# Head, last items and end of a 32-item attention and graph-convolution kernel: values, x loads, a scaling and additions rearranged

## The chip, the cores and the metric

The kernel runs on one core of a Trainium2 chip. A core has five engines that run their own instruction queues beside each other: TensorE (PE, with weight loads shown apart as PEld), VectorE (DVE), ScalarE (ACT), GpSimd (POOL) and SyncE (SP), which here only issues DMAs. The metric is the device time of one execution in microseconds, the median of several. Times of instructions come from one profiled execution.

## The reference

For 32 items x of 512 nodes by 512 features, and one 512x512 adjacency, two layers, each with a residual and a layer normalisation:

```python
q, k, v = x @ Wq + bq, x @ Wk + bk, x @ Wv + bv          # 8 heads of 64
scores  = einsum('bihd,bjhd->bhij', q, k) / 8 + mask     # -1e9 where adj == 0
out     = einsum('bhij,bjhd->bihd', softmax(scores), v)
x       = layernorm(x + out)
...
norm_adj = adj * deg_inv_sqrt[:, None] * deg_inv_sqrt[None, :]
x       = layernorm(x + norm_adj @ (x @ weight) + bias)
```

All is float32.

## The kernel before

**Products.** The three 512x512 products of an item with weights (values; keys and queries; the convolution) are made with seven half-size products instead of eight, from sums of blocks. A table such as `CHAIN` (L322) lists the seven: the bank of PSUM to multiply into, the two blocks, and what to do then: `put` a bank to its place (ACT copies) or `add` it there (DVE). `seven` (L357) turns a table into seven steps. Where it is done at two levels (`quarters_of`, L407), seven products of quarter blocks (matmuls with 128 columns) take the place of one of the seven, and three further ones (`OUTER`) have 256 columns. The quarter sums of x lie in the tail of the buffer `XT` (`xT` in the profile), made by POOL; those of the weights are in `wv_quarters` and `w1_quarters`, made by `weigh_quarter` (L255), whose fourth operation overwrites a quarter of the weights themselves.

**An item.** For item b of the loop at L898: `stretch` (L526) makes scores and numerators of one half of the heads (32 matmuls `sc`; DVE masks and clips, ACT exponentiates, POOL sums them into `acc`), then their values (`av`, 32 matmuls). DVE transposes each `av` into the single buffer `yb` (L514), and SP stores it in four DMAs to `yT` (L521). Then come the keys and queries of item b+1, the load of the value weights into `wqv` (`swap(1)`, L264; the same buffer holds the query weights and the value weights in turn), a second `stretch`, the loads of x of item b+2 (`load_x`, L123), and a stage of values of item b+1 (`values_of`, L379) together with the convolution of item b-1 (`convolve`, L706); at its end `swap(0)` loads the query weights. In the first turn there is no convolution yet, so the stage of values of item 1 stands alone. `finish` (L586) holds layer 0's end: `inverse` (1/sum), `scale` (DVE, one row block of 512 at a time) or `scale_head` (ACT, one head at a time), `add` of the residual, `measure` (statistics), `root`, `norm`, `low`, `lift`, `grow`. `fold` (L540) turns the sums `acc` on DVE. `turn` (L131) transposes x into `XT` on DVE; `combine` makes its block differences on POOL.

**Order.** DVE, ACT, POOL and PE run in the order of the program: `InOrder` (L35) pins it, and so the profile names L45 for all of them. The program writes that order by hand with `play` (L106): a list of main steps, and a dictionary of what is to be issued after which step. SP's DMAs aren't pinned: the framework places them among the others, and SP then runs its queue strictly in that order. Tiles have a fixed number of buffers in pools; a new tile waits until the old one's readers are done.

**The ends.** Item 1's weights at the start are in `wv` (part of the numerators' buffer) and are stored once to DRAM (`stored[1]`, `wv_parts` in the profile), from where `swap(1)` loads them. For the last items the schedule differs: the stage of item 30 (`b == LAST - 1`) makes the convolution of item 29 with one level (`second`), its statistics and `low` of item 30 already in that stage. After the loop follow the convolutions of items 30 and 31. In the one of item 30 the seven products are copied aside, and POOL adds them to their places later (`move`, L800; the list `extend`).

Lines the change touches: L255 to L261 `weigh_quarter`, L401 in `values_of`, L883 to L891 before the loop, L905 the first `stretch`, L926 and L937 what is beside keys and queries, L961 to L998 the stage of values, L1016 to L1019 the end.

Of the kernel before, what the change touches and what calls it, by code (L numbers as in the profile page):

```python
# [10 lines left out]
F32 = mybir.dt.float32  # L11
# [7 lines left out]
P = 128  # L19
# [31 lines left out]
def unshifted(  # L51
# [54 lines left out]
    def play(main, beside=None):  # L106
        for n, f in enumerate(main):
            f()
            run((beside or {}).get(n, ()))
# [21 lines left out]
    def turn(b, j):  # L131
        vector.transpose(
            XT[:, 2 * j : 2 * j + 2].rearrange("p i u (k s) -> p (i u) k s", s=32),
            X.pop((b, j)).rearrange("p k t r -> p t k r"),
        )
# [116 lines left out]
    w1_quarters = consts.tile([P, 3, 4, P], F32, name="w1_quarters")  # L252
    stored = [drams.tile([P, 7, 2, HALF], F32, name=f"{name}_parts") for name in ("wq", "wv", "w1")]

    def weigh_quarter(w, new, at, engine):  # L255
        old = w[:, 1:5].rearrange("p k u (r o) -> p k u r o", r=2)
        to, a, c, op = (
            (new[:, 0], old[:, :, 0, 1], old[:, :, 1, 1], ALU.add), (new[:, 1], new[:, 0], old[:, :, 0, 0], ALU.subtract),
            (new[:, 2], old[:, :, 0, 0], old[:, :, 0, 1], ALU.subtract), (old[:, :, 0, 1], old[:, :, 1, 0], new[:, 1], ALU.subtract),
        )[at]  # L260
        engine.tensor_tensor(to, a, c, op)  # L261

# [116 lines left out]
    def values_of(b):  # L379
        w = wqv if b else wv  # L380

        def multiply(p, i, j, fresh):
            for r in range(2):
                for u in range(2):
                    tensor.matmul(
                        p[:, r, :], XT[:, j, u, ts(r, P)], w[:, i, u, :],
                        start=fresh and r == 0 and u == 0, stop=u == 1, skip_group_check=True,
                    )

        def out(i, j):  # L390
            if b not in V:
                V[b] = acts.tile([P, NT, D], F32, name="v", bufs=1)
            return V[b][:, 2 * j : 2 * j + 2, ts(i, HALF)]

        def put(q, p):
            scalar.copy(out(*q), p)

        def add(q, p):
            vector.tensor_add(out(*q), out(*q), p)

        if b == 0:  # L401
            return seven(PLAIN_FIRST, multiply, put, add)
        left = lambda k, s: XT[:, s, k % 2, ts(k // 2, P)] if k in (0, 1, 3) else QUARTERS[:, max(k - 3, 0), s - 1]
        leaf, _ = quarters_of(left, w, wv_quarters, lambda: V[b], lambda: out(0, 0))
        return leaf, lambda: gpsimd.tensor_add(out(0, 1), out(0, 1), out(1, 1)), seven(OUTER, multiply, put, add)
# [474 lines left out]
    wq_parts = each(lambda k: weigh_part(wqv, vector, k), *range(4))  # L880
    kq = keys_and_queries(0, 0)
    run(wq_parts[:2] + kq[:1] + wq_parts[2:3] + kq[1:2] + wq_parts[3:] + kq[2:])
    for k in range(4):  # L883
        weigh_quarter(wv, wv_quarters, k, gpsimd)
    gather(first_rows, rows(bv))
    nc.sync.dma_start(stored[1], NUM[:, :4].rearrange("p e k (u o) -> p (e k) u o", u=2)[:, :7])
    nc.sync.dma_start(stored[0], wqv)
    play(keys_and_queries(0, 1), {
        1: [lambda: adjacency(0)], 3: [lambda: turn(1, 0), lambda: adjacency(1)],
    })  # L890
    turn(1, 1)  # L891
    for k in range(4):
        combine(1, k)

# [3 lines left out]
    for b in range(B):  # L898
# [3 lines left out]
        if b == LAST - 1:  # L902
            nc.sync.dma_start(w1[:, 1:5, 0, P:], stored[2][:, 1:5, 0, P:])
        biased = []
        stretch(b, one, back["measure"][:3] if back else ())  # L905

        def folds(gs):
            return [[lambda g=g, b=b: fold(b, g)] for g in gs]
# [9 lines left out]
        if b < LAST:  # L918
            k0, k1 = keys_and_queries(b + 1, 0), keys_and_queries(b + 1, 1)
            main = [p for pair in zip(k0, k1) for p in pair]  # L920
            if b == 0:
                exact = each(compare, *range(NT))
                weights = each(lambda k: weigh_part(w1, gpsimd, k), *range(4))
                beside = {
                    1: fold0, 2: [degrees], 3: weights[:1], 4: fold1, 5: weights[1:2] + exact[:1], 6: exact[1:2],
                    7: weights[2:3], 8: exact[2:3], 9: weights[3:], 10: exact[3:], 11: [quarters],  # L926
                    12: each(lambda k: weigh_quarter(w1, w1_quarters, k, gpsimd), *range(3)),
                }
            else:
                measure, norm, low = ahead["measure"], ahead["norm"], ahead["low"]  # L930
                loads = [lambda b=b: biased.extend(load_residual(b))]
                scale = ahead["inverse"] + ahead["scale"] if b == 1 else []
                beside = {
                    0: rest + scale + ahead["add"], 1: store[:1] + fold0, 2: store[1:2], 3: store[2:3] + fold1,
                    4: store[3:] + measure[:2] + (loads if b == LAST - 1 else []), 5: measure[2:] + ahead["root"] + [quarters],
                    7: norm[:1] + ahead["judge"], 8: norm[1:2] + low[:1] + ([lambda: run(biased)] if b == LAST - 1 else []),
                    9: norm[2:3] + low[1:2] + (loads if b < LAST - 1 else []), 10: norm[3:] + low[2:3],  # L937
                    11: low[3:] + ahead["lift_all"],
                }
            play(main, beside)  # L940
            if b == 0:
                nc.sync.dma_start(stored[2], w1)
        else:
            e = f[b]
            conv = c[b - 1]
            play(conv["first"], {
                0: rest + store[:1] + conv["parts"][:0], 1: store[1:2] + ahead["judge"] + conv["parts"][:1],
                2: store[2:] + e["sums0"],
                3: conv["parts"][1:] + e["inverse0"] + ahead["grow"],
            })  # L950
# [9 lines left out]
            load_x(b + 2, 1)  # L960
        if b < LAST:  # L961
            end = f[b]
            leaf, spread_last, outer = values_of(b + 1)
            v = leaf[:6] + outer[:1] + leaf[6:] + [spread_last] + outer[1:]
            if b == 0:
                play(v, {
                    1: fold0, 4: fold1, 9: turn0 + [lambda: weigh_quarter(w1, w1_quarters, 3, gpsimd)],
                    10: turn1 + combined[:2], 11: combined[2:] + [lambda: swap(0)],
                })
            else:  # L970
                conv = c[b - 1]
                if b < LAST - 1:
                    leaf, outer = conv["leaf"], conv["outer"]
                    main = (
                        conv["first"] + v[:10] + leaf[:6] + outer[:1] + leaf[6:] + outer[1:2] + [conv["spread_last"]]
                        + v[10:11] + outer[2:3] + v[11:] + outer[3:]
                    )
                else:
                    second = conv["second"]
                    main = conv["first"] + v[:10] + second[:1] + v[10:11] + second[1:2] + v[11:] + second[2:]  # L980
                grow, parts, scale, heads = ahead["grow"], conv["parts"], end["scale"], end["scale_heads"]
                if b < LAST - 1:
                    beside = {
                        1: parts[:1] + fold0 + grow[:2], 2: grow[2:], 3: parts[1:] + conv["unjoin"] + conv["quarters"] + fold1,
                        5: end["inverse"], 7: heads[:14], 11: heads[14:23], 13: conv["open"], 16: turn0,
                        17: heads[23:], 19: conv["join"] + turn1, 20: combined[:1] + biased[:], 24: combined[1:2],
                        26: combined[2:] + [lambda: swap(0)],
                        27: [lambda: run(conv["extend"])],
                    }
                else:  # L990
                    measure, norm, low = end["measure"], end["norm"], end["low"]
                    biased = load_residual(LAST)
                    beside = {
                        1: parts[:1] + fold0, 3: parts[1:] + fold1, 5: end["inverse"], 6: grow[:1],
                        9: grow[1:2] + scale[3:], 11: grow[2:3] + scale[:1], 13: grow[3:] + scale[1:3] + end["add"],
                        16: measure[:2], 17: measure[2:3] + measure[3:] + end["root"],
                        18: norm[:1], 19: norm[1:2] + low[:1], 20: norm[2:3] + low[1:2] + biased,
                        21: norm[3:] + low[2:3], 22: low[3:] + end["lift"],  # L998
                    }
                play(main, beside)  # L1000

# [11 lines left out]
        0: end["sums1"] + end["turn_values"] + end["inverse1"], 1: whole[0], 2: whole[1] + halves[:1], 3: whole[2],  # L1013
        4: whole[3] + halves[1:] + norm[:1], 5: low[:1] + norm[1:2], 6: low[1:2] + norm[2:3],
    })
    run(block[:1] + norm[3:] + low[2:3] + block[1:2] + low[3:] + block[2:] + end["lift"] + held["extend"])  # L1016
    run(e["unload"] + e["parts"] + end["grow"])
    s, tail, halves = e["second"], held["measure"][2:] + held["root"] + held["store"], e["halves"]
    run(s[:2] + halves[0] + s[2:4] + held["measure"][:2] + end["judge"])  # L1019
    vector.tensor_reduce(count, FINE, AX.X, ALU.add)  # L1020
    run(s[4:5] + tail[:3] + s[5:6])

# [290 lines left out]
```

## Time and profile before

| | us |
|---|---|
| median of 3 runs | 2726.34 (2726.14 to 2730.94) |
| the profiled execution | 2729.19, of which its span 2727.4 |
| first `stretch` of item 0 begins | 49.44 |
| values of item 1 (28 matmuls of 128 columns, 12 of 256) | 103.24 to 123.64 |
| an item in the middle (from one second stretch to the next) | 83.45 |
| its keys and queries; its values and convolution | 24.37; 30.9 |
| stage of values with item 30 | 2602.93 to 2635.84 |
| from the last `av` matmuls' end to the end of the span | 2674.64 to 2727.4 |

The span begins at the first instruction and ends with the last. A row of a timeline is a start, a length, an engine, a line, an operation with its output and inputs, and how often it ran in a row; in brackets stands how long the engine was idle before and what it waited for. A PE row's length includes the modelled end of its last matmul, so that rows can overlap. A float32 matmul gives two records in the trace.

### The profile page before, as it was taken

The numbers are of one execution on the slowest core, as the hardware profiler recorded it, in microseconds if no ns is written. First come the engines' busy times: TensorE is split into PE (matmuls) and PEld (weight loads), VectorE is DVE, ScalarE is ACT, GpSimd is POOL, SyncE is SP. The second block draws the span as 40 slices with busy tenths as digits, with TensorE's granted clock in tenths as the row PEclk, the third lists the DMA queues.
The fourth block names the chain that finished last, engine by engine and source line by source line (L and its number), as shares of the span: only waits on it lengthen the run. The fifth ranks groups of instructions, "written<-read, shape, count | busy, mean of one in ns | idle before, by whom it ended". The sixth has DMA issues, their size and how long they took to land. (4 is left out here: it accounts for less than half of the span.)

```text
span 2727.4 us, 39255 instructions
## 1 busy us (share of the span) xinstructions
PE 2697.1 (99%) x13980; PEld 1914.4 (70%) x13980; DVE 1960.0 (72%) x2751; ACT 1515.8 (56%) x2793; POOL 2062.6 (76%) x1385
## 2 busy tenths in 40 slices
PE   9999999999999999999999999999999999999997
PEld 6676676766767767767667677677676676766765
DVE  4777767777777777767777777777767767777777
ACT  3355555565555655555655556555556555565554
POOL 5777787777787777877777877778777787777765
PEclk9999999999999999999999999999999999999999
DMA  6335444545345454444553454544545444445541
GB/s 185 109 92 145 121 108 114 119 128 128 104 114 139 105 141 117 106 124 112 137 126 103 116 138 106 134 117 101 132 111 140 122 106 113 122 125 128 127 90 44
DMA packets 421468, 323.79 MB, mean 119 GB/s; under 512 B 279825, under 2 KB 347921, under 8 KB 413073
## 3 DMA queue, kind: packets, MB, share of 16 engines
q1 hardware_dynamic: 387520, 254.88, 31.9%
q0 software_dynamic: 32736, 65.02, 14.9%
q8 instruction: 113, 1.85, 0.3%
q10 hardware_dynamic: 1008, 1.31, 0.2%
q14 instruction: 91, 0.74, 0.1%
HBM read 248.78 MB, written 39.06 MB: 106 GB/s over the span
## 5 line engine op out<-in xcount | busy, mean ns | idle before, releaser
L45 ACT ACTIVATE e<-e 128x1024 f32<-128x1024 f32 x512 | 541.0, 1057 | 128.4 <-DVE e L45 97.5
L45 POOL TENSOR_TENSOR acc<-acc,e 128x1024 f32<-128x1024 f32 x248 | 589.3, 2376 | 19.4
L45 DVE SCALAR_TENSOR_TENSOR e<-sc,maskT 128x1024 f32<-128x1024 f32 x512 | 584.9, 1214 | 19.7 <-PE sc L45 19.4
L45 PE MATMUL mm<-xT,wk 128*128 128x256 f32 x1792 | 464.5, 382 | 2.7 <-DVE kq L45 2.5
L45 PE MATMUL mm<-xT,wqv 128*128 128x256 f32 x1792 | 459.9, 379 | 0.0
L45 PE MATMUL sc<-kq 64*128 64x512 f32 x2048 | 458.5, 596 | 0.0
L45 PE MATMUL av<-e,v 128*64 128x512 f32 x2048 | 453.6, 595 | 0.2
L45 POOL TENSOR_TENSOR xT<-xT 128x512 f32<-128x512 f32 x250 | 332.5, 1340 | 84.5 <-DVE xT L45 52.3
L45 PEld LDWEIGHTS mm<-xT,wk 128*128 128x128 f32 x1792 | 336.3, 190 | 77.1 <-DVE mv L45 23.5
L45 POOL TENSOR_TENSOR acc<-e 128x1024 f32<-128x1024 f32 x126 | 297.4, 2361 | 122.2 <-ACT e L45 122.2
L45 ACT ACTIVATE kq<-mm,bias 128x256 f32<-128x256 f32 x512 | 214.6, 473 | 295.0 <-PE mm L45 287.6
L45 PEld LDWEIGHTS mm<-xT,wqv 128*128 128x128 f32 x1792 | 340.5, 190 | 46.3
L45 POOL TENSOR_TENSOR e<-e 128x512 f32<-128x512 f32 x240 | 305.0, 1282 | 73.2 <-ACT e L45 57.0
L45 PEld LDWEIGHTS sc<-kq 64*128 64x128 f32 x2048 | 192.2, 187 | 234.7 <-issue 172.7
L45 PEld LDWEIGHTS av<-e,v 128*64 128x64 f32 x2048 | 145.5, 137 | 300.8 <-issue 234.0
L45 PE MATMUL mm<-wqv,xT 128*128 128x128 f32 (+1 forms) x1736 | 305.9, 322 | 4.6 <-DVE v L45 4.6
L45 PE MATMUL mm<-w,e 128*128 128x128 f32 (+1 forms) x1680 | 298.3, 323 | 0.5 <-DVE xT L45 0.5
L45 PEld LDWEIGHTS mm<-wqv,xT 128*128 128x128 f32 x1736 | 263.9, 192 | 27.7 <-DVE v L45 3.8
L45 DVE STREAM_TRANSPOSE yb<-av 128x512 f32<-128x512 f32 x127 | 91.0, 717 | 258.2 <-DMA yT<-yb 180.2
L45 PEld LDWEIGHTS mm<-w,e 128*128 128x128 f32 x1680 | 253.2, 191 | 26.1 <-DVE y L45 7.1
L45 DVE TENSOR_TENSOR v<-v,mm 128x512 f32<-128x512 f32 x221 | 149.0, 686 | 156.2 <-PE mm L45 78.1
L45 ACT ACTIVATE yT<-yT,inv 128x64 f32<-128x64 f32 x928 | 231.0, 337 | 0.0
(142 smaller groups left out, 3443.5 us busy)
## 6 DMA issues: line engine op xcount, KB each, us to landing
wqv<-wv_parts SPq DMA_DIRECT2D x31, 1792.0 KB, 8.7
wqv<-wq_parts SPq DMA_DIRECT2D x30, 1792.0 KB, 10.0
yT<-yb SPq DMA_DIRECT2D x508, 64.0 KB, 2.4
e<-in_x_dram SPq DMA_DIRECT2D x248, 128.0 KB, 2.7
xr<-in_L_gnn_bv_dram POOLq DMA_DIRECT2D x31, 1024.0 KB, 11.0
xr<-in_x_dram SPq DMA_DIRECT2D x122, 256.0 KB, 4.8
yT<-in_L_gnn_bias_dram POOLq DMA_DIRECT2D x30, 1024.0 KB, 12.2
out_dram<-y SPq DMA_DIRECT2D x120, 256.0 KB, 4.9
```

What stands on the lines that cost most here:

```text
L45: return self.tc.keep_in_program_order(op(*args, **kwargs))
```

## The change

Five things are changed.

1. The values of item 1 are made with one level (`CHAIN`) instead of two. The four `weigh_quarter` operations on `wv` at the start go. They are done after item 1's first value products instead, on `wqv`, which has been loaded from the stored weights without them; the fourth writes to a tile of its own, `fourth`, which SP stores over the quarter of `stored[1]` that it replaces. The quarters of x and `spread_last` are not made for item 1.
2. `turn(1, 1)`, the second transposition of x of item 1, is issued within the keys and queries of item 0, not after them.
3. The residual's load (`load_residual`, L181) is issued in the stage of values, not in the keys and queries.
4. In the stage of item 30, four `scale` operations of DVE become 32 `scale_head` operations of ACT; additions, statistics and normalisations are spread otherwise, and the last two `low` and the `lift` operations are moved into the first `stretch` of item 31.
5. At the end, POOL's two differences of block sums (`e["parts"]`) are issued before the seven additions of `extend`, and those run in the order 0, 3, 6, 1, 2, 4, 5. `judge` is issued before the first statistics of item 30.

```diff
-    def weigh_quarter(w, new, at, engine):
+    def weigh_quarter(w, new, at, engine, last=None):
...
-            (new[:, 2], old[:, :, 0, 0], old[:, :, 0, 1], ALU.subtract), (old[:, :, 0, 1], old[:, :, 1, 0], new[:, 1], ALU.subtract),
+            (new[:, 2], old[:, :, 0, 0], old[:, :, 0, 1], ALU.subtract), (old[:, :, 0, 1] if last is None else last, old[:, :, 1, 0], new[:, 1], ALU.subtract),
...
-        if b == 0:
-            return seven(PLAIN_FIRST, multiply, put, add)
+        if b < 2:
+            return seven(CHAIN if b else PLAIN_FIRST, multiply, put, add)
...
-    for k in range(4):
-        weigh_quarter(wv, wv_quarters, k, gpsimd)
...
-        1: [lambda: adjacency(0)], 3: [lambda: turn(1, 0), lambda: adjacency(1)],
+        1: [lambda: adjacency(0)], 3: [lambda: turn(1, 0), lambda: adjacency(1)], 5: [lambda: turn(1, 1)],
     })
-    turn(1, 1)
...
-        stretch(b, one, back["measure"][:3] if back else ())
+        late = ahead["low"][2:] + ahead["lift"] if b == LAST else []
+        stretch(b, one, late + back["measure"][:3] if back else ())
...
-                    7: weights[2:3], 8: exact[2:3], 9: weights[3:], 10: exact[3:], 11: [quarters],
+                    7: weights[2:3], 8: exact[2:3], 9: weights[3:], 10: exact[3:],
...
-                    9: norm[2:3] + low[1:2] + (loads if b < LAST - 1 else []), 10: norm[3:] + low[2:3],
+                    9: norm[2:3] + low[1:2], 10: norm[3:] + low[2:3],
...
             if b == 0:
-                play(v, {
-                    1: fold0, 4: fold1, 9: turn0 + [lambda: weigh_quarter(w1, w1_quarters, 3, gpsimd)],
-                    10: turn1 + combined[:2], 11: combined[2:] + [lambda: swap(0)],
+                fourth = acts.tile([P, 4, P], F32, name="fourth", tag="lo", bufs=1)
+
+                def weigh_values():
+                    for k in range(4):
+                        weigh_quarter(wqv, wv_quarters, k, gpsimd, fourth)
+                    nc.sync.dma_start(stored[1][:, 1:5, 0, P:], fourth)
+                    weigh_quarter(w1, w1_quarters, 3, gpsimd)
+
+                play(values_of(1), {
+                    0: fold0, 1: fold1 + [weigh_values], 4: turn0, 6: turn1 + combined + [lambda: swap(0)],
                 })
...
-                        1: parts[:1] + fold0 + grow[:2], 2: grow[2:], 3: parts[1:] + conv["unjoin"] + conv["quarters"] + fold1,
+                        1: parts[:1] + fold0 + grow[:2], 2: grow[2:] + loads, 3: parts[1:] + conv["unjoin"] + conv["quarters"] + fold1,
...
-                        17: heads[23:], 19: conv["join"] + turn1, 20: combined[:1] + biased[:], 24: combined[1:2],
+                        17: heads[23:], 19: conv["join"] + turn1, 20: combined[:1] + [lambda: run(biased)], 24: combined[1:2],
...
-                        1: parts[:1] + fold0, 3: parts[1:] + fold1, 5: end["inverse"], 6: grow[:1],
-                        9: grow[1:2] + scale[3:], 11: grow[2:3] + scale[:1], 13: grow[3:] + scale[1:3] + end["add"],
-                        16: measure[:2], 17: measure[2:3] + measure[3:] + end["root"],
-                        18: norm[:1], 19: norm[1:2] + low[:1], 20: norm[2:3] + low[1:2] + biased,
-                        21: norm[3:] + low[2:3], 22: low[3:] + end["lift"],
+                        1: parts[:1] + fold0 + grow[:2], 2: grow[2:], 3: parts[1:] + fold1, 5: end["inverse"],
+                        7: heads[24:] + heads[:6], 11: heads[6:24], 13: end["add"],
+                        15: measure[:1], 16: measure[1:2], 17: measure[2:3], 18: measure[3:] + end["root"],
+                        19: norm[:1], 20: norm[1:2] + low[:1], 21: norm[2:3] + low[1:2] + biased, 22: norm[3:],
...
-    run(block[:1] + norm[3:] + low[2:3] + block[1:2] + low[3:] + block[2:] + end["lift"] + held["extend"])
-    run(e["unload"] + e["parts"] + end["grow"])
+    run(block[:1] + norm[3:] + low[2:3] + block[1:2] + low[3:] + block[2:] + end["lift"])
+    run(e["unload"] + e["parts"] + [held["extend"][k] for k in (0, 3, 6, 1, 2, 4, 5)] + end["grow"])
...
-    run(s[:2] + halves[0] + s[2:4] + held["measure"][:2] + end["judge"])
+    run(s[:2] + halves[0] + s[2:4] + end["judge"] + held["measure"][:2])
```

More of the change, by code (lines that the diff above doesn't have):

```diff
@@ L962, in unshifted @@
             end = f[b]
-            leaf, spread_last, outer = values_of(b + 1)
-            v = leaf[:6] + outer[:1] + leaf[6:] + [spread_last] + outer[1:]
             if b == 0:
-                play(v, {
-                    1: fold0, 4: fold1, 9: turn0 + [lambda: weigh_quarter(w1, w1_quarters, 3, gpsimd)],
-                    10: turn1 + combined[:2], 11: combined[2:] + [lambda: swap(0)],
-                })
-            else:
+                fourth = acts.tile([P, 4, P], F32, name="fourth", tag="lo", bufs=1)
[6 more added lines that the diff above has]
+                    0: fold0, 1: fold1 + [weigh_values], 4: turn0, 6: turn1 + combined + [lambda: swap(0)],
+                })
+            else:
+                leaf, spread_last, outer = values_of(b + 1)
+                v = leaf[:6] + outer[:1] + leaf[6:] + [spread_last] + outer[1:]
                 conv = c[b - 1]
```

## The prediction

> **What bounds the kernel now.** I read the page's busy times first, then a table of stages from the TensorE timeline, then the stretches where PE is not full: the head, item 30, the end.
>
> ```profile
> PE 2697.1 (99%) x13980; PEld 1914.4 (70%) x13980; DVE 1960.0 (72%) x2751; ACT 1515.8 (56%) x2793; POOL 2062.6 (76%) x1385
> ```
>
> PE is the bound: a middle item takes 83.45 us and PE fills it. Time can only be won where PE stands or runs slowly. The first such place is the values of item 1, 103.24 to 123.64 us. Timelines of DVE, PE and SP there (start, length, work, [idle before, releaser]), then busy time by window (PE, PEld, DVE, ACT, POOL, then the granted clock):
>
> ```profile
> 105.34 0.72 DVE L45 STREAM_TRANSPOSE yb<-av 128x512 f32<-128x512 f32 x1 [4.70 <-PE mm L45]
> 114.56 0.69 DVE L45 TENSOR_TENSOR v<-v,mm 128x512 f32<-128x512 f32 x1 [1.93 <-ACT v L45]
> 119.19 0.69 DVE L45 TENSOR_TENSOR v<-v,mm 128x512 f32<-128x512 f32 x1 [2.79 <-PE mm L45]
> ```
> ```profile
> 112.78 1.13 PE L45 MATMUL mm<-wqv,xT 128*128 128x128 f32 x8 [2.07 <-DVE v L45]
> 115.30 3.78 PE L45 MATMUL mm<-wqv,xT 128*128 128x256 f32 x8 [1.40 <-DVE v L45]
> 119.94 3.78 PE L45 MATMUL mm<-wqv,xT 128*128 128x256 f32 x8 [0.85 <-DVE v L45]
> 123.64 7.47 PE L45 MATMUL sc<-kq 64*128 64x512 f32 x32
> ```
> ```profile
> 100.67 2.66 SPq L521 DMA_DIRECT2D yT<-yb  x4
> 105.91 1.68 SPq L126 DMA_DIRECT2D e<-in_x_dram  x2
> 107.69 2.65 SPq L521 DMA_DIRECT2D yT<-yb  x4
> 110.38 3.10 SPq L126 DMA_DIRECT2D e<-in_x_dram  x6
> ```
> ```profile
> 114.40:117.70 3.30, 2.40 (x6) 1.96 (x7) 1.84 (x2) 0.13 (x1) 2.50 (x2) 0.50 0.14 39
> 124.70:131.00 6.30, 6.30 (x30) 2.48 (x28) 6.18 (x7) 4.29 (x5) 3.96 (x3) 1.00 0.81 293
> ```
>
> PE waits 2.07, 1.40 and 0.85 us for additions on DVE, and its clock falls to 0.50, so that eight 128x256 records take 3.78 us instead of 1.89 (108.82). DVE is late because its second `yb` transposition, whose single buffer must be emptied by SP's four stores, starts only at 105.34.
>
> **What the skill says.** "TensorE: Matmul & The Clock Gate", Part 1: the clock halves after an idle window of about 3.4 us and returns after a busy one. The trace agrees: 0.50 from 114.4, 1.00 from 124.7, some 4.7 us after PE's last restart. "Perfetto Trace Analysis", DMA Instruction — HWDGE: the sequencer sits in its semaphore wait and is free for the next instruction only after issuing this one. SP's timeline agrees, at 2156 us: a load waits for POOL's last `yT` addition (2151.53, 4.98 long), and the store behind it, whose data ACT had ready at 2152.43, starts only after it, 4.57 us late:
>
> ```profile
> 2156.54 0.35 SPq L188 DMA_DIRECT2D xr<-in_x_dram  x1
> 2157.00 0.37 SPq L850 DMA_DIRECT2D out_dram<-y  x1
> ```
>
> **Part 1, values of item 1.** Pure PE work: 56 records of 0.216 us (12.1 us; PE's products of eight 128x256 records start 1.73 apart at full speed) against 56 of 0.1115 (eight 128x128 start 0.89 apart, 104.24 to 105.13) and 24 of 0.216 (11.4): +0.7 us, if nothing waits. What was in the way partly goes (the quarters, `spread_last`). But the fourth weight quarter is now written to a buffer and stored by SP. In the built order of SP's queue that store stands directly behind the `wqv` load, ahead of the eight `yb` stores and eight x loads shown above. It waits for POOL. POOL's order there is six accumulations, then four weight operations. From its timeline the accumulations end at
>
> ```profile
> 103.53 4.79 POOL L45 TENSOR_TENSOR acc<-acc,e 128x1024 f32<-128x1024 f32 x2
> ```
>
> 108.32; the four operations at 1.27 to 1.74 each (the same ones at the start of the kernel) end about 113.6. So SP stands still from 101 to 113.6, and the first `yb` stores begin at 113.95 (0.34 issue) instead of 100.67. The second `yb` transposition follows 4.67 later, as before: 118.6. Behind it on DVE stand two folds (2 x 2.43): 124.2, then two v additions: 125.45. PE has done six products of 1.73 by 113.6 and needs the second addition for the seventh: idle 11.8 us. The clock halves, the seventh product takes 3.46, scores of item 1 begin at 128.9, the first pair at half speed, and DVE's first masking lands at 130.4 to 131.8 against 125.16. Cost +5.9 (5.2 to 6.6). The x loads, issued until 125, land by about 127.6; their two transpositions are out of DVE's way by 129 and limit nothing. The later load of queries' weights, issued about 129, lands 10 us later, before 144.7, when it is read.
>
> The four weight operations leave POOL's start (from 22 us), where POOL is not awaited: 0.
>
> **Part 2, x turned earlier.** One DVE transposition of 1.24 us moves from ahead of the first masking into an idle gap of 0.97:
>
> ```profile
> 49.55 1.28 DVE L45 TENSOR_TENSOR kq<-kq,mm 128x512 f32<-128x512 f32 x2 [0.97 <-PE mm L45]
> 50.75 1.24 DVE L45 STREAM_TRANSPOSE xT<-e 128x1024 f32<-128x1024 f32 x1
> 51.91 1.19 DVE L45 SCALAR_TENSOR_TENSOR e<-sc,maskT 128x1024 f32<-128x1024 f32 x1
> ```
>
> The first masking starts 1.05 earlier (0.6 to 1.2), and all behind it. If the gap is gone it is worth nothing.
>
> **Part 3, residual loads.** In the 28 middle items the built order of SP, POOL and DVE is the same line for line: the loads are written elsewhere and land in the same place. 0.
>
> **Part 4, item 30.** Four DVE scalings (1.28 for two, 2.94 for two: 4.2 us, in the DVE timeline from 2616.86 and 2620.09) become 32 ACT scalings of 0.249 us (231.0 / 928 of the page), 8.0 us on an engine that has the room: ACT is busy 56%. Weight loads' timeline of that stage:
>
> ```profile
> 2624.28 1.59 PEld L45 LDWEIGHTS mm<-wqv,xT 128*128 128x128 f32 x8 [0.67 <-DVE v L45]
> 2630.20 3.32 PEld L45 LDWEIGHTS mm<-w,e 128*128 128x128 f32 x16 [0.88 <-issue]
> ```
>
> Stops of 0.67, 0.88 and 0.39 (2633.91) are all DVE's lateness and go: the scores of the last item start at 2634.1, not 2635.84; `low` no longer delays its first masking (2637.50), which comes at 2635.4. -2.1 us (-1.4 to -2.3), carried to 2674.6, since POOL's four `lift`s of 1.27, now after the accumulations, end before its next work. If ACT were late instead, the stops stay and the gain is 0.
>
> **Part 5, the end.** POOL's two `xT` operations go ahead of seven additions:
>
> ```profile
> 2706.16 1.27 POOL L45 TENSOR_TENSOR y<-yT,e 128x512 f32<-128x512 f32 x1
> 2707.38 2.62 POOL L45 TENSOR_TENSOR xT<-xT 128x512 f32<-128x512 f32 x2
> ```
>
> They can start only when DVE has made its `xT` (2699.47, 3.13 long), so the additions run 2703.3 to 2712.3 instead of 2697.86 to 2707.43. PE's wait of 1.1 us for POOL's `xT` goes, but DVE's statistics of the last rows, begun at 2711.82, wait till 2712.3. +0.5 (-0.9 to +1.6); the 7 us behind them are unchanged. "SBUF — State Buffer", Who interferes with whom, has DVE with two SBUF inputs block POOL: these `xT` operations took 1.24 to 1.56 us where additions from PSUM took 0.68, so POOL and DVE side by side could cost the upper end.
>
> **The sum.** 5.9 - 1.05 + 0 - 2.1 + 0.5 = +3.3. The profiled execution took 2729.19 (span 2727.4 and 1.8 outside it), hence 2732.5 for such an execution; the median of runs is 2726.34, hence 2729.6.
>
> **Rivals.** (a) The store doesn't hold SP's queue, or POOL's weights end early. Then `yb` is emptied as before, the values take about 12 us with DVE's chain ending near 115.5, and the head wins about 10: 2726.3 - 9 - 1.05 - 2.1 + 0.5, about 2715. For it: PE's work is dense once no addition is awaited. Against it: SP's order as built, and the 4.57 us above. (b) Slower: the clock stays at half through the scores of item 1, because after the 11.8 us pause PE, waiting on DVE at each score pair, never shows a fully busy window. 7.4 us of scores would take 13.8: +6.4, about 2736. It decides once PE's share in the windows after 125.5 is well under 1. Against: at half speed a pair takes 1.73 against DVE's 1.19, so PE is the full one, and before the clock was back 4.7 us after restart. (c) Item 30 gives nothing, as ACT is late: about 2731.7. (d) The change does not do what it says: the residual loads, if they did move, would free SP from waits like the one at 2157; then up to 6 us of waits before keys and queries, summed over 29 items, go: about 2724. Against: identical order.
>
> **Numbers.** A difference under 0.2% (5.45 us) can't be told from none. Forecast 0.70 (same 0.58, slower 0.10, faster 0.02), (a) 0.13 faster, (b) 0.09 slower, (c) 0.06 (same 0.03, slower 0.03), (d) 0.02 same: faster 0.15, same 0.63, slower 0.22. The forecast's own bounds are 4.0 to 6.0 for the head with part 2 (5.2 - 1.2 to 6.6 - 0.6), -2.3 to -1.4 and -0.9 to +1.6: 2727.1 to 2732.5; the runs of before themselves spread over 4.8. The range, 2722 to 2735, leaves out (a) and (b).
>
> **What would show it.** In the changed trace: SP's `fourth` store near 113.6 with `yb` stores behind it; DVE's second `yb` transposition near 118.6; PE idle some 12 us before the seventh product and clock 0.5 there; middle items at 83.45; no stop of weight loads in item 30; POOL's additions ending near 2712 in the old frame. It is wrong if the `yb` stores go out at 101, or if the clock stays low after 131.

## The result, and the profile after

| | before | changed kernel |
|---|---|---|
| median, us | 2729.23 of 22 runs (2724.65 to 2733.03) | 2733.99 of 22 runs (2730.95 to 2737.83) |
| ratio to before | | 1.0019, 95% interval 1.0012 to 1.0026 |
| span of the profiled execution, us | 2727.4 | 2731.3 |

The changed kernel is 0.12 to 0.26% slower. The median of before that the prediction started from, 2726.34 of three runs, was 2.9 us below that of all 22; this moves the predicted 2729.6, but not the predicted difference of 3.3.

The page of the changed kernel still shows PE as the bound:

```profile
PE 2693.9 (99%) x13956; PEld 1913.8 (70%) x13956; DVE 1955.1 (72%) x2743; ACT 1521.9 (56%) x2825; POOL 2051.8 (75%) x1380
```

PE is 3.2 us less busy and the span 3.9 longer, so the time was lost by PE standing still. Where, is seen from the starts of PE's stages in the two timelines:

| stage | before | after | difference |
|---|---|---|---|
| start to first scores of item 0 | 49.44 | 49.42 | -0.02 |
| first scores of item 0 | 8.33 | 7.27 | -1.06 |
| values of item 1 | 20.40 | 25.61 | +5.21 |
| first scores of item 1 | 7.40 | 8.28 | +0.88 |
| from there to the stage with item 30 | 2471.89 | 2471.47 | -0.42 |
| stage with item 30 | 32.90 | 31.69 | -1.21 |
| first scores of item 31 | 7.54 | 7.07 | -0.47 |
| convolution between | 10.08 | 10.06 | -0.02 |
| second scores of item 31 | 7.14 | 8.10 | +0.96 |
| end of the last `av` to the end of the span | 52.76 | 52.76 | 0.00 |
| sum | | | +3.85 |

**The head.** Timelines of SP, DVE and PE of the changed kernel (start, length, engine, line, work, times in a row, [idle before and what ended it]):

```profile
112.26 0.37 SPq L967 DMA_DIRECT2D wv_parts<-fourth  x1
112.73 2.68 SPq L521 DMA_DIRECT2D yT<-yb  x4
115.51 1.06 SPq L126 DMA_DIRECT2D e<-in_x_dram  x2
118.07 2.65 SPq L521 DMA_DIRECT2D yT<-yb  x4
```
```profile
117.33 0.72 DVE L45 STREAM_TRANSPOSE yb<-av 128x512 f32<-128x512 f32 x1 [17.75 <-DMA yT<-yb]
...
122.75 1.27 DVE L45 TENSOR_TENSOR v<-v,mm 128x512 f32<-128x512 f32 x2
...
129.91 1.23 DVE L45 SCALAR_TENSOR_TENSOR e<-sc,maskT 128x1024 f32<-128x1024 f32 x1 [0.77 <-PE sc L45]
```
```profile
102.18 10.63 PE L45 MATMUL mm<-wqv,xT 128*128 128x256 f32 x48
124.08 3.78 PE L45 MATMUL mm<-wqv,xT 128*128 128x256 f32 x8 [11.27 <-DVE v L45]
127.79 3.63 PE L45 MATMUL sc<-kq 64*128 64x512 f32 x10
```

The rows show one chain: SP issues nothing from the load at 88.19 until POOL has made `fourth`; then come the stores of `yb`, for which DVE has been idle 17.75 us; two folds later DVE makes the additions, and PE, idle for 11.27 us after six products in one dense run, starts the seventh at half speed. (The queue has nothing due until the first `yb`, which DVE makes at 98.86; from then on its standing costs.) In the table of windows (us, busy time of PE, weight loads, DVE, ACT, POOL) the granted clock is the third figure from the end of a row: 0.56, 0.50, 0.64, 1.00.

```profile
116.20:119.60 3.40, 0.00 (x0) 0.00 (x0) 2.24 (x3) 0.00 (x0) 0.00 (x0) 0.56 0.39 99
...
124.10:127.50 3.40, 3.40 (x8) 2.50 (x8) 1.80 (x2) 0.00 (x0) 0.00 (x0) 0.50 0.38 100
127.80:131.20 3.40, 3.40 (x11) 1.55 (x12) 2.53 (x3) 0.61 (x2) 1.90 (x2) 0.64 0.67 202
131.20:135.00 3.80, 3.80 (x20) 1.71 (x18) 3.80 (x4) 3.58 (x4) 3.72 (x4) 1.00 0.72 304
```

**Item 31.** Item 30's stage and the first scores of item 31 won 1.68 us; 0.96 of it is given back in the second scores of item 31. DVE, POOL and PE of the changed kernel there:

```profile
2650.64 3.64 DVE L45 SCALAR_TENSOR_TENSOR lo<-yT,dis,hi 128x512 fp32r<-128x512 f32 x2
...
2658.25 1.18 DVE L45 TENSOR_TENSOR ve<-mv,eps 128x4 f32<-128x4 f32 x1
2659.35 0.16 DVE L45 TENSOR_SCALAR nmu<-mv 128x4 f32<-128x4 f32 x1
```
```profile
2648.59 5.13 POOL L45 TENSOR_TENSOR xT<-e 128x1024 f32<-128x1024 f32 x2
2654.36 5.05 POOL L45 TENSOR_TENSOR yT<-yT,b_r 128x512 f32<-128x512 f32 x4 [0.63 <-DVE lo L45]
2659.51 1.04 POOL L45 TENSOR_TENSOR rstd<-ve,minus_half 128x4 f32<-128x4 f32 x1
```
```profile
2663.38 1.13 PE L45 MATMUL sc<-kq 64*128 64x512 f32 x4
2665.27 6.28 PE L45 MATMUL sc<-kq 64*128 64x512 f32 x28 [0.76 <-ACT zT L45]
```

The two `low` operations that were moved here take 3.64 us, where two took 1.42 in the end of before (2693.04); here POOL's accumulation runs beside them. Statistics of item 29, behind them on DVE, come later, and their root on POOL (`rstd`) stands behind the four `lift` additions, moved here as well. The lifts hold it in two ways that end together: the last lift is done at 2659.41, and DVE's `ve`, from which the root is taken, lasts beside them until 2659.43 (1.18 us, against 0.16 in before), with `nmu` behind it until 2659.51, when the root starts. ACT waits for the root, and PE for the bank of PSUM that ACT copies after it. The root starts 3.87 us ahead of the second scores, where it had 6.37 in before.

**The end.** PE's wait of 1.1 us for POOL's `xT` is gone, and a new one of 1.07 stands in its place:

```profile
2714.23 0.19 PE L45 MATMUL mm<-ones,count 128*1 128x1 f32 x2 [1.07 <-DVE count L45]
```

DVE makes `count` behind the operations of `judge` and two statistics. None of these waits for POOL, but two of `judge`'s run beside POOL's additions and take 1.8 us together:

```profile
2710.35 0.60 DVE L45 TENSOR_SCALAR low<-inv 128x32 f32<-128x32 f32 x1
2710.98 1.20 DVE L45 SCALAR_TENSOR_TENSOR low<-inv,low 128x32 f32<-128x32 f32 x1
```

In before they took 0.95 and 0.19 (2709.09). Even so `count` is done 0.5 us sooner after the last `av` than in before (35.6 against 36.1 us); it is PE that gets there earlier still. POOL's additions end at 2715.80 instead of 2707.43, and DVE's next statistics wait for them; against the last `av` these start 0.2 later than before, and DVE's last operation ends 0.2 later. That is less than what the end varies by: in before with part 1 alone and in before with SP pinned, whose ends are before's, it took 52.2 and 51.9.

### The profile page after: what moved, and what is told of

The parts are those of the page before. It is cut to its first block, busy times and chain, and to the rows that moved or that the text cites. A ratio compares the mean times of both kernels' runs of the same rounds, so it can differ in the third digit from the quotient of the medians.

```text
span 2731.3 us, 39221 instructions
## 1 busy us (share of the span) xinstructions
PE 2693.9 (99%) x13956; PEld 1913.8 (70%) x13956; DVE 1955.1 (72%) x2743; ACT 1521.9 (56%) x2825; POOL 2051.8 (75%) x1380
## 4 chain that ended last, share of the span: by engine, by line
PE 89%; POOL 3%; DVE 3%; DMA 2%; SPq 1%; issue 1%; ACT 1%; DVEq 0%; POOLq 0%; ACTq 0%
PE mm L45 58%; PE sc L45 16%; PE av L45 15%; DMA out_dram<-y 2%; POOL yT L45 1%; POOL acc L45 1%; DVE st L45 0%; SPq L188 0%; DVE ve L45 0%; SPq L521 0%; DVE lo L45 0%; DMA yT<-yb 0%; ACT e L45 0%; SPq L850 0%; POOL y L45 0%
## 5 line engine op out<-in xcount | busy, mean ns | idle before, releaser
L45 PE MATMUL mm<-wqv,xT 128*128 128x256 f32 (+1 forms) x1736 | 306.3, 323 | 11.3 <-DVE v L45 11.3
L45 ACT ACTIVATE yT<-yT,inv 128x64 f32<-128x64 f32 x960 | 238.9, 337 | 0.0
```

What stands on the lines that cost most here:

```text
L45: return self.tc.keep_in_program_order(op(*args, **kwargs))
```

## The experiments

Each was run beside the kernel before; a ratio is to that kernel.

**The store on another queue.**

```diff
-                    nc.sync.dma_start(stored[1][:, 1:5, 0, P:], fourth)
+                    gpsimd.dma_start(stored[1][:, 1:5, 0, P:], fourth)
```

> The changed kernel, with the store of the fourth quarter issued by POOL's own queue instead of SP's; nothing else differs. Theory (SP's queue stands behind that store): SP's yb stores begin near 99.6 us, DVE's second yb transposition near 104.3 instead of 117.33, PE starts the seventh product near 112.6 without a pause over 1 us and at full clock, and the first masking of item 1 starts at 115 to 117 us instead of 129.91; the whole is 12 to 14 us shorter than the changed kernel, 8 to 10 shorter than before (ratio 0.9963 to 0.9971). Rival A (the DVE chain of two folds and two additions makes PE wait in any case, the store is a bystander): the first masking stays within 2 us of 129.9. Rival B (the x loads are the real limit): PE runs dense, but the masking waits for the turned x till about 126.

Median 2721.25, ratio 0.9972 (0.9962 to 0.9983). SP, DVE and PE of this kernel:

```profile
100.09 2.65 SPq L521 DMA_DIRECT2D yT<-yb  x4
105.30 0.83 SPq L126 DMA_DIRECT2D e<-in_x_dram  x2
```
```profile
104.67 0.72 DVE L45 STREAM_TRANSPOSE yb<-av 128x512 f32<-128x512 f32 x1 [4.60 <-PE mm L45]
...
116.70 9.10 DVE L45 SCALAR_TENSOR_TENSOR e<-sc,maskT 128x1024 f32<-128x1024 f32 x8
```
```profile
102.67 12.35 PE L45 MATMUL mm<-wqv,xT 128*128 128x256 f32 x56
114.95 7.51 PE L45 MATMUL sc<-kq 64*128 64x512 f32 x32
```

The seven products are one row of 12.35 us without a stop, and the masking starts at 116.70. One line of code that says which queue carries 0.25 MB decides between 0.28% faster and 0.19% slower. The ratio is a hair above the expected 0.9963 to 0.9971. Rivals A and B fall. The theory of SP's queue is shown.

**The store where it was, but a second `yb`.**

```diff
-        yb = work.tile([P, 4, NT, 32], F32, name="yb", bufs=1)
+        if b == 0 and g == ORDER[3]:
+            yb = acts.tile([P, 4, NT, 32], F32, name="yb2", tag="hi", bufs=1)
+        else:
+            yb = work.tile([P, 4, NT, 32], F32, name="yb", bufs=1)
```

> The changed kernel with the store still in SP's queue, but the second yb of item 0's second stretch in a buffer of its own, so that DVE doesn't wait for SP there. Theory (SP's stop reaches PE through the single yb buffer first, and through the x loads behind it second): the second yb transposition at 102.5, no pause ahead of the seventh product (ends near 114.3), but the turned x is late, since its loads leave SP after 119: first masking at 126 to 127 instead of 129.91, av of item 1 at 133 to 135 instead of 136.06, so only 1 to 3.5 us are won. Rival (only yb counts): the first masking at 115 to 117, 12 to 14 us won.

Ratio 1.0009 (1.0000 to 1.0017). DVE and PE:

```profile
102.70 0.72 DVE L45 STREAM_TRANSPOSE yb<-av 128x512 f32<-128x512 f32 x1 [2.72 <-PE av L45]
...
123.55 1.25 DVE L45 STREAM_TRANSPOSE xT<-e 128x1024 f32<-128x1024 f32 x1 [11.27 <-DMA e<-in_x_dram]
...
127.23 6.84 DVE L45 SCALAR_TENSOR_TENSOR e<-sc,maskT 128x1024 f32<-128x1024 f32 x6
```
```profile
114.87 2.85 PE L45 MATMUL sc<-kq 64*128 64x512 f32 x12
125.51 2.08 PE L45 MATMUL sc<-kq 64*128 64x512 f32 x4 [7.80 <-DVE v L45]
```

PE has its seven products by 114.87, 12.9 us earlier than in the changed kernel, and then stands 7.80 us, since the additions that free the banks are queued on DVE behind a transposition of x, whose load is behind the same store on SP. `av` of item 1 start at 133.80 instead of 136.06: 2.3 won. (The masking itself, at 127.23, is 0.2 later than expected.) The rival, that only `yb` counts, falls. A stop of this queue acted through both things behind it; taking away the first wait showed the second.

**The lifts behind the roots.**

```diff
-        late = ahead["low"][2:] + ahead["lift"] if b == LAST else []
+        late = ahead["low"][2:] if b == LAST else []
...
-                0: rest + store[:1] + conv["parts"][:0], 1: store[1:2] + ahead["judge"] + conv["parts"][:1],
+                0: rest + ahead["lift"] + store[:1] + conv["parts"][:0], 1: store[1:2] + ahead["judge"] + conv["parts"][:1],
```

> The changed kernel with POOL's four lift additions of item 30 moved from the first stretch of item 31 to behind the roots of item 29's statistics; the two low operations stay. Theory (the 0.96 us that item 31's second scores lost comes from the roots, and so ACT's copies, standing behind the lifts on POOL): POOL's rstd about 1.1 us earlier against the scores of item 31, the second scores take 7.1 to 7.3 us instead of 8.10, 0.8 to 1.0 us won. Rival (the low operation that DVE made beside POOL's accumulation, 3.64 us for two, decides alone): ACT stays late and the second scores stay at 7.9 or more.

Ratio 1.0015 (1.0008 to 1.0023), not to be told from the changed kernel's. PE, DVE and POOL:

```profile
2664.00 7.20 PE L45 MATMUL sc<-kq 64*128 64x512 f32 x32
```
```profile
2658.91 0.16 DVE L45 TENSOR_TENSOR ve<-mv,eps 128x4 f32<-128x4 f32 x1
```
```profile
2659.15 1.04 POOL L45 TENSOR_TENSOR rstd<-ve,minus_half 128x4 f32<-128x4 f32 x1 [4.77 <-DVE nmu L45]
...
2672.91 6.98 POOL L45 TENSOR_TENSOR wqv<-e 128x1024 f32<-128x1024 f32 x3
```

The scores of item 31 start 0.64 later in this execution, so the root is 1.0 earlier against them, and the second scores take 7.15 without a stop: the place of the lifts was the cause, although `low` still takes 3.65. The microsecond is that of `ve`, which is back at 0.16; the root follows `nmu` at once here too. The root's lead over the scores is 4.85 us, still less than in before, but enough. But POOL's last accumulations now end at 2679.89, 1.7 after the last `av`, where in before they ended with it and in the changed kernel 0.5 after, and DVE's sixteen scalings there take 7.23 instead of 6.01. From the last `av` to PE's first product with `parts` it takes 6.03 instead of 5.21: 0.82 of the 0.95 is given back at once, and the rest is too small for the whole time to show.

**SP's queue in the order of the program.** The framework put the residual's loads back where they had been: in the two traces SP issues its 1100 DMAs in the same order, with the one new store added. Here SP's `yb` stores, x loads, residual loads and output stores are pinned as the engines' work is:

```diff
-    tensor, vector, scalar, gpsimd = (InOrder(tc, e) for e in (nc.tensor, nc.vector, nc.scalar, nc.gpsimd))
+    tensor, vector, scalar, gpsimd, sync = (InOrder(tc, e) for e in (nc.tensor, nc.vector, nc.scalar, nc.gpsimd, nc.sync))
...
-            nc.sync.dma_start(R[b][i], x[b, ts(i, P), :])
+            sync.dma_start(R[b][i], x[b, ts(i, P), :])
```

and so for the other three.

> The changed kernel with SP's yb stores, x loads, residual loads and output stores kept in the order of the program, so that the residual's loads really move into the stage of values (behind the x loads, ahead of the query weights). Theory that part 3 as built moves nothing, and that the waits ahead of keys and queries (4.3 us summed over 28 middle items in the changed kernel, 5.8 before) come from output stores standing behind residual loads: the stages of keys and queries all take 24.37 to 24.45, 3.5 to 4.5 us won. Rival (they come from something else, or the 1 MB of loads now collides with the x loads or the weights): the sum of these waits stays at 4 us or more, or a wait of over 0.1 us per item appears in the stage of values.

Median 2728.38, ratio 1.0000 (0.9992 to 1.0009), against 1.0019 of the changed kernel. The waits ahead of keys and queries, summed over 28 items from the starts of PE's stages:

| kernel | sum of waits, us | largest |
|---|---|---|
| before | 5.80 | 1.03 |
| changed | 4.25 | 1.08 |
| changed, pinned | 0.02 | 0.00 |
| before, pinned (below) | 0.02 | 0.00 |

The keys and queries of the last item, not in this sum, wait 0.24 us in before, 0.88 in the changed kernel and not at all in the pinned ones. With it the changed kernel's waits are 5.1 us, and 0.0019 of the ratio is 5.2. In the stage of item 30, on the other hand, pinning the changed kernel made a stop ahead of `folded` longer (0.59 us), and the stage took 32.18 instead of 31.69.

How such a wait comes about is to be seen in the changed kernel, in the stage with the largest. POOL, SP, DVE, PE:

```profile
1905.86 4.98 POOL L45 TENSOR_TENSOR yT<-yT,xr 128x512 f32<-128x512 f32 x4
```
```profile
1910.86 0.35 SPq L188 DMA_DIRECT2D xr<-in_x_dram  x1
1911.31 0.38 SPq L850 DMA_DIRECT2D out_dram<-y  x1
```
```profile
1921.55 0.75 DVE L45 SCALAR_TENSOR_TENSOR lo<-yT,dis,hi 128x512 fp32r<-128x512 f32 x1 [5.07 <-DMA out_dram<-y]
```
```profile
1922.96 1.13 PE L45 MATMUL mm<-xT,wk 128*128 128x256 f32 x4 [0.81 <-DVE kq L45]
```

A residual load waits for POOL to be done with the old residual (1910.84). The output store behind it goes late, `lo`, which takes the store's buffer, later still, and the additions of keys and queries are behind `lo` on DVE. In the pinned kernel the four output stores stand alone, ahead of any residual load:

```profile
2153.20 4.62 SPq L45 DMA_DIRECT2D out_dram<-y  x4
...
2194.08 1.82 SPq L45 DMA_DIRECT2D xr<-in_x_dram  x4
```

**Part 1 alone**, on the kernel before:

> The kernel before with part 1 alone (item 1's values with one level, the fourth quarter stored by SP). Theory (part 1 carries the whole loss): the stage of values begins at 103.2 as before and takes 25.4 to 25.8 us instead of 20.40, the second scores of item 1's turn start 6.0 to 6.3 us later than before (168.7 to 169.0 instead of 162.66), and nothing of it comes back: about 6 us slower (ratio 1.0015 to 1.0030). Rival (the loss at the head needs the earlier turn of x as well, or comes from elsewhere): under 3 us later at that point.

Ratio 1.0025 (1.0016 to 1.0035). The stage of values took 25.62 and the scores after it 7.23. The point at 162.66 came at 168.88; but this execution's first scores had begun 1.17 later already (50.61), so part 1 costs 5.05 to there, a microsecond less than expected. The ratio fits the changed kernel's: 1.0025 here times the 0.9992 of the other parts (next run) is 1.0017, against 1.0019. The whole loss is in part 1, as the theory has it; the difference is in the scores at half clock, 7.23 here and 8.28 in the changed kernel.

**Parts 2, 4 and 5 alone**, on the kernel before:

> The kernel before with parts 2, 4 and 5 alone (x turned earlier, item 30's scaling on ACT, the end's order). Theory: the av of item 0 start 1.05 earlier (56.7 instead of 57.76) and this lasts to 162 us (161.6); item 30's stage takes 31.6 to 32.2 instead of 32.90 and the first scores of item 31 7.07 instead of 7.54, but its second scores 8.1 instead of 7.14; from their av's end to the span's end 52.6 to 53.0 as before (52.76). In all 1.3 to 2.2 faster plus the middle's waits, which vary by 1 to 2 us: ratio 0.9985 to 1.0000. Rival (the loss in item 31's second scores comes from the head's delay or from part 1): its second scores take 7.1 to 7.3.

Median 2725.36, ratio 0.9992 (0.9985 to 0.9999). The first scores took 7.27 instead of 8.33. Item 30's stage took 31.37, the first scores of item 31 7.07, its second 8.09, the end 52.6. Each is as the theory says (the stage 0.2 better), and the loss in item 31 is there without part 1. Rival fallen.

**The kernel before with SP pinned**, nothing moved in the program:

> The kernel before, unchanged in what is issued where in the program, but SP's yb stores, x loads, residual loads and output stores kept in the program's order: the output stores then all stand ahead of the residual's loads in the stage of keys and queries. Theory (an output store waiting behind a residual load that waits for POOL is what delays low, and so keys and queries): the summed waits of 5.8 us fall to under 0.5, ratio 0.9975 to 0.9985, without part 3. Rival (only loads that lie in the stage of values free the stores, or the 1 MB in that stage collides with the weights' load and costs a new wait): the sum stays over 3 us, or values lose over 0.1 us per item.

Median 2722.67, ratio 0.9978 (0.9969 to 0.9987), waits 0.02. Part 3 isn't needed for it: with the loads where they were, the stores are ahead of them once SP keeps to the program.

**All that helped, together**: the changed kernel with POOL's store, the second `yb`, SP pinned, and `count` summed ahead of item 30's statistics.

> The changed kernel with the fourth quarter stored by POOL's queue, the second yb of item 0 in a buffer of its own, SP's stores and loads in the program's order, and the count of the last checks summed ahead of the statistics of item 30. Theory (the gains add, as they lie in different stages): first masking of item 1 at 114.5 to 117, summed waits of keys and queries under 0.3, so 13 to 15 us at the head and 4 to 6 in the middle below the changed kernel: ratio to before 0.9938 to 0.9958. Rival (a shorter head makes the weights' or x's loads late, or the waits return): ratio 0.9965 or more.

Median 2713.89, ratio 0.9946 (0.9933 to 0.9960), faster than both kernels. The first masking is at 117.05, in an execution whose first scores began 1.30 later than in before; waits 0.02; item 31's second scores still 8.14. PE doesn't wait for `count` any more, but the end takes 52.1, as it did in the pinned kernel without that move, so nothing is owed to it.

## Why the prediction was right or wrong

- **The sum** was right in sign and near in size: +3.3 predicted, +3.9 between the two profiled executions, +4.8 between medians, of which the interval, 3.3 to 7.1, holds the 3.3 at its edge. That it came so near is in part luck: part 4 brought 1.4 us less than forecast, against which stand 0.5 from part 5 and 0.4 from the waits of the middle, which weren't forecast and differ between executions. The median of 2733.99 lies outside the forecast's own 2727.1 to 2732.5, which start from three runs that were 2.9 us low; only the stated range of 2722 to 2735 holds it.
- **Part 1** was right in mechanism and time of each step: store 113.6 predicted (112.5 in the frame shifted by part 2), 112.26 measured; idle 11.8, 11.27 measured; cost 5.9, and 5.21 + 0.88 = 6.1 measured. But the cost isn't one number. Over four executions with this same stall, stage and scores together cost 4.7 (25.38 + 7.13, the kernel with the lifts moved), 5.05, 5.35 (25.58 + 7.57, SP pinned) and 6.1, each against the 27.80 of the one execution of before. In the 8 us from the start of the seventh product the granted clock averaged 0.80, 0.75, 0.70 and 0.61 in these, which is 3.2, 4.0, 4.8 and 6.2 us at half clock. Half of the 3.0 between the extremes is 1.5, and the costs differ by 1.4: when the clock returned accounts for the difference. The Trainium skill, "TensorE: Matmul & The Clock Gate", Part 1, says why that can be: its windows run freely, so that the time until the clock returns depends on where in one the work starts. It puts the variation at half a microsecond either way; here it is three times that. The kernel before isn't free of it either: with SP pinned, stage and scores took 26.48 (19.28 + 7.20), at a mean clock of 0.76 instead of 0.63 over 14 us of it. So 4.7 lies outside the stated 5.2 to 6.6, and that the profiled execution came within 0.2 of 5.9 is luck.
- **The clock in before.** The prediction says that its halving at 114.4 agrees with that page's idle window of 3.4 us. There was none: the window from 111.00 to 114.40 still has a clock of 0.96 and 1.13 us of PE work in it, and PE's longest stop until then was 2.07. In this trace a window that was one third busy did not keep the clock. The stall of 11.27 us, where the clock was 1.00 from 112.80 to 116.20 and fell after that, does agree.
- **Part 2** was right: 1.05 predicted, 1.06 measured.
- **Part 3**: nothing, as the identical order of SP's queue said, before and after; it was not run by itself. Rival (d), that moved loads would free up to 6 us, was right as a mechanism (0.0019 of the ratio, 5 us, in the changed kernel; 0.0022, 6 us, in before), and right to be put aside for this change.
- **Part 4**, predicted -2.1, brought -1.21 - 0.47 + 0.96 = -0.7. Two terms failed. The stops of 0.67, 0.88 and 0.39, in sum 1.94, were read from the weight loads' idle time. The starts of PE's own rows in before (below) give less: 0.42, 0.66 and 0.43 more than the 1.73 that eight records need, in sum 1.5; the third lies within the last row. All three went; without part 1 the stage won just that, 1.53. In the changed kernel it won 1.21, since PE stopped for 0.26 ahead of `folded` (2616.99), which DVE makes behind a late `yb`. And "carried to 2674.6, since POOL's four `lift`s of 1.27, now after the accumulations, end before its next work" was wrong: their next work is the root of item 29's statistics, which ACT, and behind ACT PE, waited for. The lifts cost 0.95 there, by holding DVE's `ve` as much as by standing ahead of the root. I had looked at POOL's accumulations for the next reader and not at its small operations.

```profile
2624.28 1.99 PE L45 MATMUL mm<-wqv,xT 128*128 128x256 f32 x8 [0.27 <-DVE v L45]
2630.23 5.68 PE L45 MATMUL mm<-w,e 128*128 128x256 f32 x24 [0.50 <-DVE xT L45]
```

- **Part 5**, predicted +0.5 (-0.9 to +1.6), brought 0.0 between these two executions and 0.2 up to DVE's last operation. The additions ended at 2711.9 in the frame of before (2715.80 - 3.9), as predicted near 2712.3. That "PE's wait of 1.1 us for POOL's `xT` goes" was only half so: `count` took its place.
- **Rivals**: (a) did not happen, and the first experiment shows that it would have, with the store elsewhere: 0.9972, with a masking at 116.70 where 115.5 was named for the chain. (b) did not: the clock was back by 131.2. (c) did not: the stage of item 30 gained 1.21, and PE waited for ACT nowhere in it.

## What to carry to other kernels

On SP's queue here, a DMA that waited for a slow engine stopped everything behind it; before adding one, read the queue's built order and name each entry behind it and who waits for that. A short rule: let the engine that makes the data issue the store, or keep the queue in an order in which nothing that can wait stands ahead of what is due. And of work moved to fill a gap on an engine, look for the smallest instruction behind it and beside it, not only the longest: a root of 1 us, and a sum of 128x4 on DVE ahead of it, held PE here.

## What was not expected of the hardware

- The same stall of PE, some 11 us, cost from 4.7 to 6.1 us in four executions, as the clock stayed at half for 3.2 to 6.2 us after it.
- A tiny DVE operation can take as long as one of POOL's: `ve<-mv,eps` on 128x4, with both inputs in SBUF, took 1.18 us beside POOL's lifts and 0.16 with POOL idle (2653.87, before). The Trainium skill, "SBUF — State Buffer", Who interferes with whom, has a DVE operation with two inputs in SBUF contend with a POOL operation that reads SBUF, through an exclusive lock. The trace agrees: `ve` ended at 2659.43, the last lift at 2659.41.
- POOL's own store of 0.25 MB kept it busy 0.84 us (113.06, the first experiment) and delayed nothing that PE waits for.
